# A selective scan on one core: delta transposed alone and multiplied with u by tokens; softplus in two ScalarE operations

## The chip, the cores and the metric

The kernel runs on one core of a Trainium2 chip. A core has five engines with an instruction stream each: TensorE (PE, matrix products and transposes into PSUM; its weight loads are shown as PEld), VectorE (DVE), ScalarE (ACT), GpSimd (POOL) and SyncE (SP), which here issues every DMA. Each engine works through its own stream in order; engines wait for each other through semaphores. The metric is the device time of one execution in microseconds (us), median over several runs. Everything is computed in 32-bit floats.

## The reference, cut to what matters

The input is a batch of eight images of 64 x 64 tokens with 192 channels. Two layers with residual follow each other. Layer 0 (a Mamba-2 block with convolutions and an MLP) is left alone by the change. Layer 1 is a selective scan in four directions:

```python
# layer 1; b images, L = 64*64 tokens, D_INNER = 384, D_STATE = 16, DT_RANK = 12, K = 4
xz = einsum('bhwc,dc->bhwd', group_norm(x), in_proj_w)
xc, z = split(xz, 2, axis=-1)
xc = silu(depthwise_conv3x3(xc) + conv_b)              # channels first
xs = stack([rows_first(xc), columns_first(xc)])        # two orders of the tokens
xs = concatenate([xs, flip(xs, axis=-1)])              # and both backwards: 4 directions
x_dbl = einsum('bkdl,kcd->bkcl', xs, x_proj_weight)    # 12 + 16 + 16 rows
dts, B, C = x_dbl[:, :, :12], x_dbl[:, :, 12:28], x_dbl[:, :, 28:]
delta = softplus(einsum('bkrl,kdr->bkdl', dts, dt_projs_weight) + dt_projs_bias)
A = -exp(A_logs)
def step(h, (d, b, c, u)):                             # token by token, u is xs
    h = exp(d[..., None] * A) * h + (d * u)[..., None] * b
    return h, sum_n(h * c)
y = sum over the directions, each turned back, of (scan(step) + xs * D)
out = x + (layer_norm(y) * silu(z)) @ out_proj_w.T
```

What the change touches is delta, the product d * u, and how the latter gets into the layout in which it is multiplied with B.

## The kernel before

Layer 0 runs over the eight images first and leaves its result in DRAM (`x1s`). Then layer 1 goes image by image. The 384 channels are three blocks of 128 (`DT`, index d), the 4096 tokens eight chunks of 512 (`NT`, index c or t).

For every image there is a **front**, a **scan** and a **finish**. The front of an image and the finish of the one before it are scheduled together by a small planner (`Flow`): each is a set of generators that yield steps with an engine, a weight in us and the instructions; the planner keeps a free time for each engine and emits the step that can start first. `take` and `give` are buffer slots, `wait` is an event, `fork` starts a further generator. The weights set only the order; on the chip the engines wait for data. The wait for "front" (line 1645) is where the prologue of the scan goes on when the whole front has been planned.

- Front (lines 1110 to 1235): load x1 (L1124), project to the inner channels (PE, L1139), copy into a padded image (ACT, L1169), convolve with nine taps on one ACT and eight DVE instructions of 128 x 4096 (L1190, L1200), silu in two halves (ACT, L1213), store by channels to DRAM as `xo[0]` (L1218), and turned to columns first (ACT copy L1227) as `xo[1]` (L1230). The weights scaled with the group norm of the image (`wxz`, L1100) lie in a pool that lives through the layer.
- Finish (lines 1237 to 1389): layer norm of `yacc` (PE means L1247, DVE L1255 and L1290, ACT L1265, L1283, L1284, L1297), the gate z (PE L1327, ACT L1345, DVE L1357), the output product (PE L1374), residual (DVE L1383) and store (L1386).

The scan of an image has 32 **steps** (4 directions k of 8 chunks; directions 2 and 3 backwards), and each step 24 **units**: eight pairs of states p times three channel blocks d. The main loop (`main`, line 1693) is written out by hand; in each engine the instructions stand in the order of the program. Unit u issues, in this order: `run(u)`, two DVE scans hs of 512 tokens (L1596) and on POOL the carry cy (L1608) and the product hc = hs * C (L1610); `decay(u + 2)`, two ACT exponentials ea (L1569); two or three `weigh`, ACT operations that multiply duT, delta * u with tokens on the partitions, with one column of B (pw, L1554); `supply(u + 1)`, eight PE transposes of pw into PSUM (g, L1580); `collect(u - 1)`, PE products that sum hc over the states (y, L1625); `add(u - 2)`, which adds y to `yacc` after the last pair (L1634, L1636). cb is C repeated over the partitions (DMA, L1542), dr is delta repeated (DMA, L1536).

While a step is scanned, the next one is prepared (`prepare`, line 1420): the table that it returns (line 1508) says in which of the 24 units each piece is issued. The pieces share a single PSUM bank, so each waits until the one before has been read. In unit 0 the chunk xc of `xo[k % 2]` is loaded (L1428); units 2 to 7 make dts, B and C (L1439 to L1462); then for each block d:

```python
step:    p_dt = wd^T x_dbl                        # PE, L1468
soft:    a = |p_dt|; a = exp(-a); a = ln(a + 1)   # ACT, L1475, L1476, L1477 (tile spa)
delta:   de = max(p_dt, 0) + a                    # DVE, L1482
times_u: du = de * xc                             # POOL, L1489
turn:    four transposes of du into PSUM (p_du)   # PE, L1495
keep_du: duT = p_du                               # DVE copy, L1502
```

For the first step of an image the same pieces run as generators of the planner (`prologue`, `prologue_of`, lines 1643 to 1691).

Of the kernel before, what the change touches and what calls it, by code (L numbers as in the profile page):

```python
# [8 lines left out]
F32 = mybir.dt.float32  # L9
AF = mybir.ActivationFunctionType  # L10
# [5 lines left out]
L = HI * WI  # L16
# [15 lines left out]
EXPLN = "natural_log_exp_and_others"  # L32

# [996 lines left out]
def layer1(tc, consts, x1s, mv1, out, w_in, w_x, w_dt, w_out):  # L1030
    nc = tc.nc
    ident, low, up, grp, eps, ones96, ones1, p96, p128 = consts
# [5 lines left out]
    with ExitStack() as ctx:  # L1038
# [48 lines left out]

        wxz = [wp.tile([CP, CT, DIN], F32, name=f"wi1{n}") for n in "xz"]

# [3 lines left out]
        def scaled(f, b, half):  # L1093

            for ct in range(CT):
                r = yield step(
                    "ACT",
                    0.6,
                    lambda: [
                        nc.scalar.activation(  # L1100
                            wxz[half][:, ct],
                            wi[:, ct, half * DIN : half * DIN + DIN],
                            AF.Copy,
                            scale=sc[:, b * CT + ct : b * CT + ct + 1],
                        )
                    ],
                )
            return r

        def front(f, cx, mq, b, xo):  # L1110

            fp = cx.enter_context(tc.tile_pool(name="fr1", bufs=1, reuse_waits="tile"))
            pads = [fp.tile([128, HI + 2, WI + 2], F32, name=f"pad{i}") for i in range(2)]
            for tag, n in (("xl", 3), ("fx", 2), ("pad", 2), ("xs", 2), ("xt", 1)):
                f.pool(tag, n)
            got = {}

            def load():
                for d in range(DT):
                    for t in range(NT):  # L1120
                        tk = slice(t * TT, t * TT + TT)
                        yield "take", "xl"
                        xl = got["xl", d, t] = fp.tile([CP, CT, TT], F32, name="xl1", bufs=3)
# [3 lines left out]
            def project():  # L1127
                yield from scaled(f, b, 0)
                for d in range(DT):
                    for t in range(NT):  # L1130
# [9 lines left out]
                                    ps, wxz[0][:, ct, d * 128 : d * 128 + 128], xl[:, ct], start=ct == 0, stop=ct == 1  # L1140
# [66 lines left out]
            def store():  # L1207
                for d in range(DT):
                    yield "wait", ("conv", d)
                    xs = got["xs", d]  # L1210
                    for h in range(2):
# [12 lines left out]
                        )  # L1224
                    yield "take", "xt"
                    xt = fp.tile([128, WI, HI], F32, name="xt1")
                    r = yield step("ACT", 7.2, lambda: [nc.scalar.copy(xt, xs.rearrange("p h w -> p w h"))])  # L1227
                    f.give("xs", r + 5)
# [4 lines left out]
                f.at["front"] = r  # L1233
# [3 lines left out]
        def finish(f, cx, mq, b):  # L1237

            fp = cx.enter_context(tc.tile_pool(name="fi1", bufs=1, side="right", reuse_waits="tile"))
            full = [128, DT, TT]  # L1240
            for tag, n in (("sq", 1), ("rs", 2), ("z", 2), ("xl2", 3)):
                f.pool(tag, n)
# [72 lines left out]
            def gate():  # L1315
                yield from scaled(f, b, 1)
                for t in range(NT):
                    yield "wait", ("xl2", t)
                    xl = got["xl2", t]
                    for d in range(DT):  # L1320
# [7 lines left out]
                                    ps, wxz[1][:, ct, d * 128 : d * 128 + 128], xl[:, ct], start=ct == 0, stop=ct == 1  # L1328
# [72 lines left out]
        def scan(xo):  # L1401
# [18 lines left out]
            def prepare(s, bank=lambda name: mp.tile([128, TT], F32, name=name, tag="mm")):  # L1420
# [5 lines left out]
                def load():  # L1426
                    st["xc"] = pools["pr1"].tile([128, DT, TT], F32, name="xc")
                    o(nc.sync.dma_start(out=st["xc"], in_=xo[k % 2][:, :, c * TT : c * TT + TT]))  # L1428
                    if first(s):
                        st["wd"] = pools["pr1"].tile([45, DIN], F32, name="wd")  # L1430
                        o(nc.sync.dma_start(out=st["wd"][32:45], in_=w_dt[k]))
                    else:
                        st["wd"] = state[s - 1]["wd"]
# [39 lines left out]
                def soft(d):  # L1473
                    st["sp", d] = a = pools["pr1"].tile([128, TT], F32, name="spa", tag="tmp")
                    o(nc.scalar.activation(a, st["p_dt", d], AF.Abs))  # L1475
                    o(nc.scalar.activation(a, a, AF.Exp, scale=-1.0))  # L1476
                    o(nc.scalar.activation(a, a, AF.Ln, bias=1.0))  # L1477

                def delta(d):
# [3 lines left out]
                            st["de", d], st["p_dt", d], 0.0, st["sp", d], ALU.max, ALU.add  # L1483
                        )
                    )

                def times_u(d):
                    st["du", d] = pools["pr1"].tile([128, TT], F32, name="du", tag="tmp")
                    o(nc.gpsimd.tensor_mul(st["du", d], st["de", d], st["xc"][:, d]))  # L1489

                def turn(d):
                    st["p_du", d] = pt = bank("p_du")
                    for j in range(NB1):
                        o(
                            nc.tensor.transpose(  # L1495
                                pt[:, j * 128 : j * 128 + 128], st["du", d][:, j * 128 : j * 128 + 128], ident
# [3 lines left out]
                def keep_du(d):  # L1500
                    o(
                        nc.vector.tensor_copy(  # L1502
                            st["duT"][:, :, d * 128 : d * 128 + 128],
                            st["p_du", d].rearrange("p (j t) -> p j t", j=NB1),
                        )
# [12 lines left out]
                    10: [(soft, 1), (times_u, 0)],  # L1518
                    11: [(delta, 1), (turn, 0), (repeat_delta, s, 0)],
                    12: [(keep_du, 0), (step, 2), (times_u, 1)],  # L1520
                    13: [(soft, 2)],
                    14: [(delta, 2), (turn, 1)],
                    15: [(keep_du, 1), (times_u, 2)],
# [148 lines left out]
            def prologue_of(f, d):  # L1672
# [5 lines left out]
                yield step("ACT", 1.9, lambda: ready["soft"](d), None, "explog")  # L1678
# [4 lines left out]
                yield "take", "tmp"  # L1683
                r = yield step("POOL", 1.3, lambda: ready["times_u"](d), r)
                yield "take", "mm"
                r = yield step("PE", 0.6, lambda: ready["turn"](d))
                f.give("tmp", r)
# [42 lines left out]
        for b in range(nb + 1):  # L1730
# [8 lines left out]
            if b < nb:  # L1739
                xo = [ddp.tile([128, DT, L], F32, name=f"xo{i}") for i in range(2)]  # L1740
                chains += front(f, fr_x, mq, b, xo)
# [16 lines left out]
def tile_kernel(ctx, tc, x, p96_in, p128_in, rows, w_in0, w_out0, w_fc1, w_fc2, w_in1, w_x, w_dt, w_out1, out):  # L1758
# [10 lines left out]
    for name in ("cw1", "cw2"):  # L1769
# [4 lines left out]
    low = cp.tile([128, 128], F32, name="low")  # L1774
    make_lower_triangular(nc, low, diag=False)
    up = cp.tile([128, 128], F32, name="up")
    nc.gpsimd.memset(up, 1.0)
    nc.gpsimd.affine_select(
        out=up, in_=up, compare_op=ALU.is_ge, fill=0.0, base=0, pattern=[[1, 128]], channel_multiplier=-1
    )  # L1780
# [5 lines left out]
    ones96 = cp.tile([CP, CP], F32, name="ones96")  # L1786
    nc.gpsimd.memset(ones96, 1.0 / C)
    ones1 = cp.tile([128, 128], F32, name="ones1")
# [3 lines left out]
    nb = x.shape[0]  # L1792
    mv1 = cp.tile([CP, nb, CT, 2], F32, name="mv1")
    x1s = [dp.tile([C, L], F32, name=f"x1_{b}") for b in range(nb)]
    layer0(tc, consts, x, x1s, mv1, w_in0, w_out0, w_fc1, w_fc2, rows)
    layer1(tc, consts, x1s, mv1, out, w_in1, w_x, w_dt, w_out1)
# [58 lines left out]
```

## Time and profile before

| | |
|---|---|
| runs | 24181.09, 24186.39, 24191.97 us; median 24186.39 |
| profiled execution | 24176.65 us, span 24174.9 us, mean granted PE clock 0.972 |
| busy share of the span | PE 87%, PEld 42%, DVE 88%, ACT 89%, POOL 70% |
| mean busy share of the 16 DMA engines | 23.4% |
| layer 0 | from the start to some 4861 us |
| scans of the first image | 5056 to 7220 us; the second 7456 to 9612 us |
| costliest groups (busy us, mean ns of one) | POOL hc L1610: 14577.7, 2373; DVE hs L1596: 13069.7, 1263; ACT pw L1554: 8875.8, 601; ACT ea L1569: 8123.2, 709; PE g L1580: 6793.2, 280; PE y L1625: 6658.3, 620 |
| loads and stores (KB each) | xc 768, xo<-xs 1024, xo<-xt 2048, cb 128, dr 128 |

How to read the lines that follow: a group is named by its line, engine, operation and `out<-in` (tiles without their numbers, partitions x elements), with the count after x; then come the busy time in us and the mean of one in ns, and the idle time of the engine just before these instructions with what ended it. A timeline has start and length in us. A window has, for each engine, busy us and the number of instructions in a stretch of the span. A wait has the waiting instruction, the one that released it, the total in us, how often, and the longest. Instructions of one engine overlap a little at their ends, so lengths add up to more than the time from one start to the next.

### The profile page before, as it was taken

The page shows a single profiled execution, that of the slowest core. Times are in us where ns is not written, and L with a number is a line of the kernel's source. Part 1 is how long each engine was busy: PE and PEld are TensorE (multiplying, and loading weights), DVE is VectorE, ACT ScalarE, POOL GpSimd, SP SyncE. Part 2 cuts the span into 40 slices and gives each one's busy share as a digit, 9 for nine tenths or more (in the row PEclk, how much of TensorE's full clock was granted, in tenths as well). Part 3 has the DMA queues.
Part 4 walks back from the last instruction along what each step waited for, and adds up shares of the span by engine and source line. Part 5 has one row for each costly group of instructions (what it writes and reads, how often), then busy time and mean ns, then how long its engine had stood idle before and what let it go on. Part 6 is the DMA issues. An engine that isn't in the chain of part 4 may idle for free.

```text
span 24174.9 us, 313055 instructions
## 1 busy us (share of the span) xinstructions
PE 20986.5 (87%) x100036; PEld 10182.8 (42%) x100036; DVE 21386.3 (88%) x22093; ACT 21415.5 (89%) x38076; POOL 16907.4 (70%) x13639
## 2 busy tenths in 40 slices
PE   7999999978888888888888888888888888888888
PEld 4444444434443444344434443444344434443444
DVE  7888888779998998899889988998899989998998
ACT  5666766679998999899989998999899989998998
POOL 1111111159986998699869986998699779977997
PEclk8999999989999999999999999999999999999999
DMA  2111111122222222222222222222222222222222
GB/s 49 44 44 44 49 44 42 36 86 67 68 66 87 68 67 68 89 66 66 69 87 68 68 68 86 67 68 70 84 68 67 76 78 67 68 75 82 67 67 58
DMA packets 1129702, 1608.05 MB, mean 67 GB/s; under 512 B 259360, under 2 KB 458432, under 8 KB 1118848
## 3 DMA queue, kind: packets, MB, share of 16 engines
q1 hardware_dynamic: 1128064, 1588.03, 23.4%
q8 instruction: 806, 13.21, 0.2%
q14 instruction: 832, 6.82, 0.1%
HBM read 1024.65 MB, written 160.17 MB: 49 GB/s over the span
## 4 chain that ended last, share of the span: by engine, by line
POOL 53%; PE 25%; issue 8%; DVE 6%; ACT 5%; DMA 2%; SPq 1%; POOLq 0%; DVEq 0%; ACTq 0%
POOL hc L1610 47%; POOL cy L1608 4%; PE y L1625 3%; PE p_f L953 3%; DVE xs L1200 3%; PE p_f L973 2%; PE p_x L445 2%; PE g L1580 2%; ACT pw L1554 2%; DMA xc<-xo 2%; PE p_o L870 1%; POOL du L1489 1%; ACT ea L1569 1%; PE p_y L787 1%; PE p_d L1439 1%
## 5 line engine op out<-in xcount | busy, mean ns | idle before, releaser
L1610 POOL TENSOR_TENSOR hc<-hs,cb 128x1024 f32<-128x1024 f32 x6144 | 14577.7, 2373 | 10.3 <-POOL cy L1608 6.7
L1596 DVE TENSOR_TENSOR_SCAN hs<-ea,cy,g 128x512 f32<-128x512 f32 x10752 | 13069.7, 1263 | 783.2 <-PE g L1580 468.3
L1554 ACT ACTIVATE pw<-duT,bt 128x384 f32<-128x384 f32 x16384 | 8875.8, 601 | 11.6 <-DVE duT L1502 11.6
L1625 PE MATMUL y<-hc,sel 128*64 128x512 f32 x24576 | 6658.3, 620 | 2229.1 <-POOL hc L1610 2221.3
L1569 ACT ACTIVATE ea<-dr,an 128x512 f32<-128x512 f32 x12288 | 8123.2, 709 | 159.9 <-DVE hs L1596 131.9
L1580 PEld LDWEIGHTS g<-ident,pw 128*128 128x128 f32 x49152 | 5309.6, 141 | 4320.1 <-issue 2676.5
L1580 PE MATMUL g<-ident,pw 128*128 128x128 f32 x49152 | 6793.2, 280 | 32.4 <-DVE hs L1596 12.9
L1625 PEld LDWEIGHTS y<-hc,sel 128*64 128x64 f32 x24576 | 1229.6, 135 | 3648.1 <-POOL hc L1610 3385.1
L1489 POOL TENSOR_TENSOR du<-de,xc 128x512 f32<-128x512 f32 x768 | 982.9, 1280 | 1632.9 <-DVE de L1482 1618.2
L1608 POOL COPY cy<-hs 128x2 f32<-128x2 f32 x6144 | 1161.7, 189 | 1324.4 <-DVE hs L1596 1211.9
L1596 DVE TENSOR_TENSOR_SCAN hs<-ea,g 128x512 f32<-128x512 f32 x1536 | 1777.0, 1204 | 178.7 <-PE g L1580 138.3
L362 POOL TENSOR_TENSOR s<-xs 96x512 f32<-96x512 f32 x64 | 121.0, 1891 | 2033.2 <-DVE xs L340 1522.3
L1200 DVE SCALAR_TENSOR_TENSOR xs<-pad,p,xs 128x4096 f32<-128x4096 f32 x192 | 860.8, 4484 | 37.6 <-ACT xs L1190 30.4
L1468 PE MATMUL p_dt<-xdbl,wd 13*128 13x512 f32 x1536 | 856.8, 639 | 41.7 <-DVE de L1482 39.7
L362 POOL TENSOR_TENSOR s<-sq 96x512 f32<-96x512 f32 x128 | 210.3, 1643 | 961.7 <-ACT sq L375 890.7
L1439 PE MATMUL p_d<-xc,wx 128*44 128x512 f32 x1536 | 792.2, 598 | 95.0 <-DMA xc<-xo 95.0
L340 DVE SCALAR_TENSOR_TENSOR x<-xx,p,x 96x512 f32<-96x512 f32 x1024 | 784.4, 814 | 19.4 <-ACT x L329 19.4
L953 PE MATMUL p_f<-h,wf 96*128 96x512 f32 x1536 | 764.1, 633 | 24.4 <-ACT zs L547 14.0
L340 DVE SCALAR_TENSOR_TENSOR xs<-xin,p,xs 96x512 f32<-96x512 f32 x1024 | 749.5, 768 | 4.6 <-ACT xs L329 4.6
L1482 DVE SCALAR_TENSOR_TENSOR de<-p_dt,spa 128x512 f32<-128x512 f32 x768 | 524.1, 682 | 254.0 <-ACT spa L1477 253.0
L973 PE MATMUL p_f<-m,wf 128*96 128x512 f32 x1536 | 693.3, 602 | 0.0
L1495 PEld LDWEIGHTS p_du<-ident,du 128*128 128x128 f32 x3072 | 323.1, 141 | 743.2 <-POOL du L1489 500.3
(201 smaller groups left out, 19729.0 us busy)
## 6 DMA issues: line engine op xcount, KB each, us to landing
cb<-cd SPq DMA_DIRECT2D x4096, 128.0 KB
dr<-de SPq DMA_DIRECT2D x3072, 128.0 KB
xc<-xo SPq DMA_DIRECT2D x256, 768.0 KB
e<-csd SPq DMA_DIRECT2D x256, 384.0 KB
xl<-x SPq DMA_DIRECT2D x256, 384.0 KB
xo<-xs SPq DMA_DIRECT2D x48, 1024.0 KB
xo<-xt SPq DMA_DIRECT2D x24, 2048.0 KB
xl<-in_x SPq DMA_DIRECT2D x64, 384.0 KB
```

The lines of the kernel that those rows point to most:

```text
L340: nc.vector.scalar_tensor_tensor(im(out[:, ct]), tap(ct, j), w[:, ct, j : j + 1], im(out[:, ct]), ALU.mult, ALU.add)
L953: nc.tensor.matmul(ps, wf1[:, ct, mt * 128 : mt * 128 + 128], h[:, ct], start=ct == 0, stop=ct == 1)
L973: nc.tensor.matmul(ps[:CP], wf2[:, kt, ct * CP : ct * CP + CP], m[:, kt], start=kt == 0, stop=kt == 5)
L1200: nc.vector.scalar_tensor_tensor(xs, tap(j), kw[:, d, j : j + 1], xs, ALU.mult, ALU.add)
L1489: o(nc.gpsimd.tensor_mul(st["du", d], st["de", d], st["xc"][:, d]))
L1554: nc.scalar.activation(st["pw", p, j][:, :, i], st["duT"][:, j].rearrange("p (g c) -> p g c", c=64), AF.Copy, scale=st["bt"][:, j, n : n + 1],
L1569: nc.scalar.activation(ea[:, f], state[s]["dr", d][:, f], AF.Exp, scale=an[:, k, p, at : at + 1])
L1580: nc.tensor.transpose(g[:, f, j * 128 : j * 128 + 128], state[s]["pw", p, j][:, 2 * d + f].rearrange("p a b -> p (a b)"), ident,)
L1596: nc.vector.tensor_tensor_scan(rev(h[:, f]), rev(ea[:, f]), rev(g[:, f]), 0.0 if first(s) else state[s - 1]["cy"][:, p, d, f : f + 1], ALU ...
L1608: o(nc.gpsimd.tensor_copy(st["cy"][:, p, d], h[:, :, last]))
L1610: o(nc.gpsimd.tensor_mul(hc, h, bc(st["cb", p], 1, [128, 2, TT])))
L1625: o(nc.tensor.matmul(y[half[f]], sel, hc[:, f], start=p == 0 and k > 0, stop=p == NP1 - 1))
```

## The change

For each image the front also writes u by tokens: after each silu half a generator `by_tokens` transposes it in groups of 512 tokens on PE, ACT copies each group out of PSUM, and SP stores it to a third DRAM tensor `xo[2]` of 4096 tokens x 384 channels. At each step `load` brings the chunk in as `ut`, tokens on the partitions, in the token order of the direction: one DMA in directions 0 and 2, two in directions 1 and 3, which go through the image by columns. `turn` transposes delta itself; `keep_du`, which was a copy out of PSUM, multiplies by `ut` on the way. `times_u` on POOL and its tile du are gone, and with them the entries of units 10, 12 and 15. softplus becomes Exp and Ln, ln(exp(v) + 1), on ACT; delta is max(min(that, 60), v).

Room in SBUF is made for it: the scaled weights go into pools of the front and of the finish, xl1 has two buffers in place of three, wd one in place of two, and the constants that only layer 0 uses are in a pool that is closed after layer 0.

```diff
 def layer1(tc, consts, x1s, mv1, out, w_in, w_x, w_dt, w_out):
...
-        wxz = [wp.tile([CP, CT, DIN], F32, name=f"wi1{n}") for n in "xz"]
...
         def front(f, cx, mq, b, xo):
...
+            wx_b = fp.tile([CP, CT, DIN], F32, name="wx1b")
...
-            for tag, n in (("xl", 3), ("fx", 2), ("pad", 2), ("xs", 2), ("xt", 1)):
+            for tag, n in (("xl", 2), ("fx", 2), ("pad", 2), ("xs", 2), ("xt", 1), ("xq", 2)):
...
-                        xl = got["xl", d, t] = fp.tile([CP, CT, TT], F32, name="xl1", bufs=3)
+                        xl = got["xl", d, t] = fp.tile([CP, CT, TT], F32, name="xl1", bufs=2)
...
+                        f.fork(by_tokens(d, h, xs, r))
                     yield "take", "xt"
                     xt = fp.tile([128, WI, HI], F32, name="xt1")
                     r = yield step("ACT", 7.2, lambda: [nc.scalar.copy(xt, xs.rearrange("p h w -> p w h"))])
-                    f.give("xs", r + 5)
+                    if last := f.part(("xs", d), 3, r + 5):
+                        f.give("xs", last)
...
-                f.at["front"] = r
+                if last := f.part("front", 2 * DT + 1, r):
+                    f.at["front"] = last
+
+            def by_tokens(d, h, xs, r):
+                xf = xs.rearrange("p h w -> p (h w)")
+                for g in range(h * NT // 2, h * NT // 2 + NT // 2):
+                    yield "take", "fx"
+                    ps = mq.tile([128, TT], F32, name="p_xq", tag="fx", bufs=2)
+                    r = yield step(
+                        "PE",
+                        0.6,
+                        lambda: [
+                            nc.tensor.transpose(
+                                ps[:, j * 128 : j * 128 + 128], xf[:, g * TT + j * 128 : g * TT + j * 128 + 128], ident
+                            )
+                            for j in range(NB1)
+                        ],
+                        max(r, f.now),
+                    )
+                    yield "take", "xq"
+                    xq = fp.tile([128, NB1, 128], F32, name="xq1", bufs=2)
+                    q = yield step("ACT", 0.6, lambda: [nc.scalar.copy(xq.rearrange("p j c -> p (j c)"), ps)], r)
+                    f.give("fx", q)
+                    dst = xo[2][g * TT : g * TT + TT, d * 128 : d * 128 + 128].rearrange("(j p) c -> p j c", p=128)
+                    q = yield step("SP", 0.1, lambda: [nc.sync.dma_start(out=dst, in_=xq)], q)
+                    f.give("xq", q + 2)
+                if last := f.part(("xs", d), 3, r):
+                    f.give("xs", last)
+                if last := f.part("front", 2 * DT + 1, q):
+                    f.at["front"] = last
...
                 def load():
                     st["xc"] = pools["pr1"].tile([128, DT, TT], F32, name="xc")
                     o(nc.sync.dma_start(out=st["xc"], in_=xo[k % 2][:, :, c * TT : c * TT + TT]))
+                    st["ut"] = pools["pr1"].tile([128, NB1, DIN], F32, name="ut", bufs=1)
+                    if k % 2 == 0:
+                        src = xo[2][c * TT : c * TT + TT].rearrange("(j p) m -> p j m", p=128)
+                        o(nc.sync.dma_start(out=st["ut"], in_=src))
+                    else:
+                        for i in range(2):
+                            src = xo[2].rearrange("(h w) m -> w h m", w=WI)[c * RT + i : c * RT + RT : 2]
+                            o(nc.sync.dma_start(out=st["ut"][i * 64 : i * 64 + 64], in_=src.rearrange("j h m -> h j m")))
...
                 def soft(d):
                     st["sp", d] = a = pools["pr1"].tile([128, TT], F32, name="spa", tag="tmp")
-                    o(nc.scalar.activation(a, st["p_dt", d], AF.Abs))
-                    o(nc.scalar.activation(a, a, AF.Exp, scale=-1.0))
+                    o(nc.scalar.activation(a, st["p_dt", d], AF.Exp))
                     o(nc.scalar.activation(a, a, AF.Ln, bias=1.0))
...
-                            st["de", d], st["p_dt", d], 0.0, st["sp", d], ALU.max, ALU.add
+                            st["de", d], st["sp", d], BIG, st["p_dt", d], ALU.min, ALU.max
...
-                def times_u(d):
-                    st["du", d] = pools["pr1"].tile([128, TT], F32, name="du", tag="tmp")
-                    o(nc.gpsimd.tensor_mul(st["du", d], st["de", d], st["xc"][:, d]))
...
-                                pt[:, j * 128 : j * 128 + 128], st["du", d][:, j * 128 : j * 128 + 128], ident
+                                pt[:, j * 128 : j * 128 + 128], st["de", d][:, j * 128 : j * 128 + 128], ident
...
-                        nc.vector.tensor_copy(
+                        nc.vector.tensor_mul(
                             st["duT"][:, :, d * 128 : d * 128 + 128],
                             st["p_du", d].rearrange("p (j t) -> p j t", j=NB1),
+                            st["ut"][:, :, d * 128 : d * 128 + 128],
...
-                    10: [(soft, 1), (times_u, 0)],
+                    10: [(soft, 1)],
                     11: [(delta, 1), (turn, 0), (repeat_delta, s, 0)],
-                    12: [(keep_du, 0), (step, 2), (times_u, 1)],
+                    12: [(keep_du, 0), (step, 2)],
                     13: [(soft, 2)],
                     14: [(delta, 2), (turn, 1)],
-                    15: [(keep_du, 1), (times_u, 2)],
+                    15: [(keep_du, 1)],
...
                 xo = [ddp.tile([128, DT, L], F32, name=f"xo{i}") for i in range(2)]
+                xo.append(ddp.tile([L, DIN], F32, name="xo2"))
```

## The prediction

> **What bounds the kernel now.** I read the busy shares of the page first: ACT 89%, DVE 88%, PE 87%. Averages so near each other name no limit, so I cut out a stretch of eighteen whole steps of the scan in one batch (directions 1 to 3) and asked the windows view for each engine's busy time in it.
>
> ```profile
> core 0: us, PE busy (x) PEld busy (x) DVE busy (x) ACT busy (x) POOL busy (x), PEclk, DMA share, GB/s
> 8344.90:9560.60 1215.70, 1042.80 (x5684) 512.62 (x5685) 1138.46 (x1062) 1208.94 (x2177) 1138.43 (x918) 1.00 0.24 67
> ```
>
> A step lasts 1215.70/18 = 67.54 us. Of it ACT works 67.16, DVE 63.25, POOL 63.25, PE 57.93. ACT has 0.38 us free in a step: it is the bound there. The chain of waits on the page puts 47% on the POOL product hc instead; POOL is idle 4.3 us in each step, so I believe the windows. The waits of the same stretch say how closely the others follow (releaser, us in total, times, longest):
>
> ```profile
> DVE hs L1596 <- PE g L1580: 40.2, 58, 1.5
> DVE de L1482 <- ACT spa L1477: 16.2, 34, 0.8
> DVE hs L1596 <- ACT pw L1554: 11.7, 17, 0.7
> DVE hs L1596 <- POOL cy L1608: 7.3, 17, 0.4
> ```
>
> DVE waits for ACT (16.2 + 11.7)/18 = 1.55 us in a step, and (40.2 + 7.3)/18 = 2.64 us for PE and POOL. The second sum doesn't go away with a faster ACT; it is the second floor: 63.25 + 2.64 = 65.89 us.
>
> Between two batches (some 235 us from the last scan to the next) ACT is not the bound:
>
> ```profile
> 7220.00:7300.00 80.00, 79.14 (x182) 34.23 (x182) 50.73 (x18) 44.87 (x49) 0.66 (x3) 0.98 0.42 114
> 7300.00:7387.00 87.00, 49.28 (x92) 18.10 (x92) 84.98 (x29) 45.92 (x34) 0.00 (x0) 0.82 0.35 131
> 7387.00:7456.00 69.00, 62.58 (x149) 24.26 (x150) 29.26 (x28) 50.08 (x63) 3.80 (x3) 0.93 0.46 143
> ```
>
> Columns as above. First PE (79 of 80), then the convolutions on DVE (85 of 87, PE free for 38 us), then PE again with 6 us free.
>
> **Part 1, softplus in two operations.** The timeline of ACT shows one softplus (start, duration):
>
> ```profile
> 8374.40 0.58 ACT L1475 ACTIVATE spa<-p_dt 128x512 f32<-128x512 f32 x1
> 8375.01 0.63 ACT L1476 ACTIVATE spa<-spa 128x512 f32<-128x512 f32 x1
> 8375.68 0.63 ACT L1477 ACTIVATE spa<-spa 128x512 f32<-128x512 f32 x1
> 8376.21 1.32 ACT L1569 ACTIVATE ea<-dr,an 128x512 f32<-128x512 f32 x2
> ```
>
> From its start to the next instruction's start it takes 8376.21 - 8374.40 = 1.81 us. Abs goes, and Exp reads PSUM in Abs's place. If Exp from PSUM lasts as Abs did, 0.61 us start to start are left before Ln: saved 0.66. If it keeps its own 0.63, saved 0.61. The group means below (575 against 630 ns) follow the place read, so I take 0.66: three a step, 1.98 us; the other end is 1.83. Over 256 steps that is 507 (468) us, if ACT stays the bound. The Trainium skill, page "ScalarE: Activation LUTs", section "What ACT_TABLE_LOAD costs", gives 186 ns + 0.833 ns an element and 93 ns of overlap with the next: an estimate of 0.52 us for the removed operation and 399 us in all; but the overlap it states is not there in these rows, where each operation needs the one before it, so the rows decide.
>
> ACT's floor becomes 67.16 - 1.98 + 0.38 = 65.56 us a step, DVE's is 65.89. The later one sets the step: 67.54 - 65.89 = **1.65 us saved**, not 1.98. Above it lies 1.98 (the 2.64 shrinks too, because POOL loses du, below). Below it I set 0.90 (16.2/18): the waits for spa go, those for pw only change their name to PE or POOL. The 32 steps of a batch include eight of the first direction, with two more PE products a unit; I give them the same. 256 x 1.65 = 422 us (230 to 507).
>
> **Part 2, the product with u moves from POOL to where delta leaves PSUM.** The rows of the groups view (busy, mean ns, idle before):
>
> ```profile
> L1489 POOL TENSOR_TENSOR du<-de,xc 128x512 f32<-128x512 f32 x768 | 982.9, 1280 | 1632.9 <-DVE de L1482 1618.2 <-PE p_du L1495 9.5 <-DMA dr<-de 5.2
> ...
> L1482 DVE SCALAR_TENSOR_TENSOR de<-p_dt,spa 128x512 f32<-128x512 f32 x768 | 524.1, 682 | 254.0 <-ACT spa L1477 253.0
> L1502 DVE COPY duT<-p_du 128x512 f32<-128x512 f32 x768 | 511.0, 666 | 8.1 <-PE p_du L1495 8.1
> ...
> L1475 ACT ACTIVATE spa<-p_dt 128x512 f32<-128x512 f32 x768 | 442.0, 575 | 69.8 <-PE p_dt L1468 69.6
> ...
> L1636 DVE TENSOR_TENSOR yacc<-yacc,y 128x512 f32<-128x512 f32 x576 | 382.0, 663 | 25.7 <-PE y L1625 25.7
> ```
>
> POOL loses 3 x 1.28 us a step. POOL is no bound, so directly nothing; but each du stands ahead of an hc, and PE's y waits for that hc. That is what can take the gain past 1.65, up to 1.98. DVE's copy (666 ns) becomes a product of a PSUM and an SBUF tensor; the addition into yacc has just these operands and this size and takes 663: price 0. The dearest row of a product of this size is du's own on POOL, 1280: that is the upper end, 3 x 0.61 = 1.84 us a step. I take 663, the same engine and operands. Max-add becoming min-max leaves delta at 682.
>
> The Trainium skill speaks against this edit: page "VectorE: DVE Perf Modes", section "Mode 2×_2P — use both read ports for one tensor", says that a copy can stream one tensor over both read ports and a two-tensor operation can't. By the headline alone a product would cost twice the copy, an estimate of 768 x 0.67 = 512 us on DVE, and the gain would be gone. The same section keeps the double rate to sources in SBUF; the copy here reads PSUM, and the trace has it at the addition's 666 against 663.
>
> delta is transposed directly, so PE's turn waits for DVE's de and no longer for POOL: same four transposes, earlier by 1.28. PE is in order, with y and g behind it, so this can only help. The new wait is keep_du's for ut; behind it on DVE stand the scans.
>
> **Part 3, ut from DRAM.** Each step loads 128 x 4 x 384 x 4 bytes = 768 KB more, as large as xc, with one SP issue (two in directions 1 and 3) of some 0.6 us. On the SP queue of the gap 2816 KB (xt, then xc) go from 7396.70, the issue of xt, to 7408.32, where the first piece of the chain below ends: 11.6 us, about 250 GB/s, so 3.2 us a step, 5% on a DMA share of 24%. It is issued in unit 0 of 24 and read in unit 12, 33 us later, and no cb load is due sooner than three units (8 us) after it: hidden, 0. Without that cover it would be 3.2 us a step.
>
> **Part 4, the front.** Each batch transposes xs for it: 24 groups of four PE transposes (0.65 us as p_du's), 24 ACT copies from PSUM (0.58), 24 stores of 256 KB. Two thirds belong to channel blocks 0 and 1 and fall under the next convolution, where PE has 38 us free and ACT 41: 0. The last eight groups come after the last silu, in the third window, where the chain reads:
>
> ```profile
> 7398.35 9.97 DMA xc<-xo
> ...
> 7408.46 1.91 PE p_d L1439 x2
> ...
> 7435.01 0.70 DVE duT L1502
> ...
> 7436.25 4.64 ACT pw L1554 x9
> ...
> 7443.89 10.55 PE p_o L1374 x24
> ```
>
> There they add 8 x 0.65 = 5.3 us of PE, 4.7 of ACT, and 2 MB (8.5 us at 250 GB/s) ahead of xc on the SP queue. Against that: xc has slack, since pw ends at 7440.9 and the first g waits for the p_o of the previous batch until 7454.4; PE is free 6 us; and the POOL stage of du leaves the chain (3 us, 7432 to 7435). Ends: 5.3 + 8.5 = +14 all exposed, -3 all covered. I take **+4**, near PE's share, since PE ends this window: 8 x 4 = 32 us. The first batch has no previous one to hide behind, and xl has two buffers in place of three: its eight projections go from some 1.9 us to (3.0 load + 1.9)/2 = 2.5 each, 5 more; with 1 for the later start of the weights 6 us, once. Constants moved to another pool issue nothing new: 0.
>
> **Sum.** The profiled execution took 24176.65 us (span 24174.9 and 1.75 around it): 24176.65 - 422 + 32 + 6 = 23793. It lay 9.7 under the median of the runs, so the forecast for the median is **23802 us**.
>
> **Rivals.**
> A: ACT keeps the bound and the front is covered: 24176.65 - 507 + 9.7 = 23679, with -3 us in each of eight batches 23655. For it: POOL's 3.8 us freed. Against: DVE's floor of 65.89.
> B: DVE, PE and POOL close the gap: 0.90 a step (230) and +14 a batch (118): 24176.65 - 230 + 118 + 9.7 = 24074. For it: DVE's waits for g, 2.2 us a step, are the largest already. Against: the spa and pw waits name ACT.
> C, slower: the product at L1502 costs more on DVE than the addition shows. DVE's floor rises by three times the excess; the gain of 1.65 less the front's 38/256 = 0.15 is used up at 0.50 us each, that is from 1.17 us for one product. At du's 1280 ns: 1.84 - 1.65 + 0.15 = +0.34 a step, 87 us: 24273. For it: no product of these operands exists yet. Against: L1636.
> D: the change doesn't do what it says: Exp from PSUM lasts as long as Abs and Exp did together. Then only the front's 38 us are left: 24224. Against: ACT reads p_dt from PSUM in 575 ns now, and Exp from SBUF takes 630.
>
> **Chances.** Forecast 0.58 (its own range 23690 to 23920), A 0.12, B 0.17, C 0.10, D and what lies between B and no change 0.03. Range 23650 to 24060: A's best to near B's end. A measurement of this kernel tells about 0.2% (48 us) from no change: faster 0.84 (forecast, A and most of B), same 0.06, slower 0.10.
>
> **What would show it.** In the same stretch: a step of 65.9, ACT at 65.2 or nearly full, the spa and pw waits under half, L1502 near 665, no ut among the releasers of DVE; after the last silu eight transposed groups and the first scan some 4 us later than now. A step above 67, a product over 1.2 us, or a DMA wait at keep_du would make it wrong.

## The result and the profile after

| | median of the runs, us | lowest to highest | ratio to the kernel before, 95% interval |
|---|---|---|---|
| before | 24187.47 (4 runs) | 24181.09 to 24191.97 | |
| after | 23754.53 (4 runs) | 23741.9 to 23765.26 | 0.9821 (0.9809 to 0.9833) |

The change saves 433 us, 1.8%. The forecast was 23802, 47 us above. The profiled execution of after took 23759.13 us, its span 23757.4 against 24174.9: 417.6 us less. The instruction records give these parts of the difference:

| part of the span | before | after | difference | forecast |
|---|---|---|---|---|
| eight scans, first to last scan instruction of an image | 8 x 2164.7 | 8 x 2101.1 | -509 | -422 |
| seven gaps between two scans | 7 x 238.7 | 7 x 249.0 | +72 | +28 |
| start of the first scan | 5049.5 | 5067.5 | +18 | +10 |
| after the last scan | 137.0 | 138.3 | +1 | 0 |

By these records the first image's scan before runs from 5049.5 to 7217.1 us and the second's from 7456.5 to 9620.4. Of the 18 us, 6.6 already lie ahead of layer 1, which starts at 4861.5 us before and at 4868.1 in after; in a second run of after it starts at 4847.0, so this lies within the spread of layer 0 between runs and is none of the change's. Both large terms were missed, in opposite directions.

The windows view of after, for eighteen whole steps of directions 1 to 3 in one batch (columns: us, then busy time and instructions of PE, PEld, DVE, ACT and POOL, the PE clock, the DMA share, GB/s):

```profile
8286.40:9466.70 1180.30, 1039.59 (x5690) 512.54 (x5690) 1131.87 (x1063) 1175.85 (x2126) 1080.42 (x864) 1.00 0.31 81
```

A step is 1180.30/18 = 65.57 us, 1.97 less than the 67.54 of the same view before. ACT works 65.32 of it, DVE 62.88, POOL 60.02. By this line alone ACT, 99.6% full, is still the bound; the run without Ln below shows that a second limit lies just beside it. The waits view of the same stretch (us in total, times, longest):

```profile
PE y L1663 <- POOL hc L1648: 134.0, 252, 1.1
POOL cy L1646 <- DVE hs L1634: 90.2, 210, 1.0
...
DVE hs L1634 <- PE g L1618: 35.2, 52, 1.3
...
DVE hs L1634 <- POOL cy L1646: 6.8, 16, 0.4
...
DVE hs L1634 <- ACT pw L1592: 2.7, 5, 0.8
DVE hs L1634 <- ACT ea L1607: 1.5, 3, 0.5
```

PE's y waits 134.0 us for hc, against 163.3 before. The waits of DVE for spa are gone and those for pw fell from 11.7 to 2.7. What is left of DVE's waits is 46.2/18 = 2.57 us a step; with its 62.88 busy that is 65.45, a hair under the step. No ut stands among the releasers. The groups of the changed operations, in the groups view of the whole span (busy us, mean ns of one, idle before):

```profile
L1539 DVE TENSOR_TENSOR duT<-p_du,ut 128x512 f32<-128x512 f32 x768 | 510.1, 666 | 1.2 <-PE p_du L1532 1.2
...
L1258 ACT COPY xq<-p_xq 128x512 f32<-128x512 f32 x192 | 110.5, 584 | 168.6 <-DMA xo<-xq 167.7 <-PE p_xq L1249 0.2
```

The product costs DVE what the copy cost, 666 ns. The new copies of the front, however, wait 167.7 us for their stores, over the eight images. The gap between the first two images, in the windows view with the cuts about where one image's PE stage ends and the convolutions end:

```profile
7174.00:7252.00 78.00, 78.00 (x179) 33.88 (x176) 48.13 (x18) 43.57 (x52) 0.49 (x3) 0.97 0.40 106
7252.00:7342.00 90.00, 64.86 (x166) 28.59 (x165) 87.73 (x29) 57.16 (x50) 0.00 (x0) 0.81 0.53 182
7342.00:7422.00 80.00, 69.94 (x177) 29.25 (x177) 28.05 (x28) 53.13 (x69) 0.00 (x0) 0.87 0.52 159
```

The first two windows are about as long as before (80 and 87); the third, after the last convolution, was 69 us and is 80. The instruction records say the same without hand-made cuts, as means of the seven gaps: from the last scan instruction to the end of the convolutions 165.5 us against 167.1 before, and from there to the next scan 83.5 against 71.6. So the whole lengthening lies behind the last convolution. No engine is full in the third window. Its chain of waits shows who sets it:

```profile
7344.44 6.67 DMA xo<-xq
...
7352.53 8.74 DMA xo<-xq
...
7369.81 6.13 DMA xc<-xo
```

Two stores of transposed groups, 15 us together, now stand in the chain ahead of the load of xc.

### The profile page after: what moved, and what is told of

Same layout as the page of the kernel before. It is cut to its first block, busy times and chain, and to the rows that moved or that the text cites. A ratio compares the mean times of both kernels' runs of the same rounds, so it can differ in the third digit from the quotient of the medians.

```text
span 23757.4 us, 313126 instructions
## 1 busy us (share of the span) xinstructions
PE 21089.6 (89%) x100804; PEld 10279.5 (43%) x100804; DVE 21274.2 (90%) x22093; ACT 21040.0 (89%) x37507; POOL 16067.4 (68%) x12871
## 4 chain that ended last, share of the span: by engine, by line
POOL 43%; PE 24%; ACT 15%; DVE 7%; issue 6%; DMA 4%; SPq 1%; POOLq 0%; ACTq 0%; DVEq 0%
POOL hc L1648 40%; ACT pw L1592 6%; ACT ea L1607 6%; POOL cy L1646 3%; PE p_f L956 3%; DMA xc<-xo 2%; DVE xs L1202 2%; PE p_f L976 2%; PE p_x L448 2%; PE y L1663 2%; PE p_o L873 2%; PE p_y L790 1%; PE g L1618 1%; PE p_d L1481 1%; PE p_z L531 1%
## 5 line engine op out<-in xcount | busy, mean ns | idle before, releaser
L1532 PEld LDWEIGHTS p_du<-ident,de 128*128 128x128 f32 x3072 | 323.5, 141 | 610.2 <-DVE de L1523 405.8
L448 PE MATMUL p_x<-h,wi 96*128 96x512 f32 x1024 | 544.5, 664 | 12.3 <-ACT h L405 11.1
L365 POOL TENSOR_TENSOR s<-x 96x512 f32<-96x512 f32 x64 | 96.2, 1502 | 626.3 <-DVE x L343 477.2
```

## Experiments

Each kernel ran beside the kernel before on the same chip; ratios are to that. "Step" is the median in directions 1 to 3, "scan" the mean of the eight images' scans, "gap" the mean of the seven gaps.

| run | median us | ratio, 95% interval | step | scan | gap |
|---|---|---|---|---|---|
| before | 24162 to 24191 in four sets of runs | 1 | 67.64 | 2164.7 | 238.7 |
| after | 23754.53 | 0.9821 (0.9809 to 0.9833) | 65.57 | 2101.1 | 249.0 |
| softplus alone (e1) | 24080.99 | 0.9963 (0.9948 to 0.9978) | 67.16 | 2149.2 | 243.3 |
| move alone (e2) | 24201.65 | 1.0013 (1.0003 to 1.0022) | 67.34 | 2157.6 | 248.9 |
| after, again | 23747.24 | 0.9824 (0.9807 to 0.984) | 65.56 | 2101.3 | 250.0 |
| softplus alone, du not awaited (e8) | 24093.41 | 0.9969 (0.9958 to 0.9981) | 67.16 | 2152.2 | 242.9 |
| the same, half of du (e15) | 23821.18 | 0.9845 (0.9828 to 0.9861) | 66.24 | 2117.3 | 242.9 |
| after without Ln (e6) | 23699.04 | 0.9805 (0.9791 to 0.982) | 65.55 | 2095.9 | 249.3 |
| after, ut loaded once (e9) | 23759.48 | 0.9818 (0.9803 to 0.9833) | 65.57 | 2100.4 | 250.3 |
| after, four xq buffers (e3) | 23703.71 | 0.9807 (0.9792 to 0.9821) | 65.57 | 2100.6 | 245.2 |
| the same again (e3b) | 23710.31 | 0.9801 (0.9786 to 0.9815) | 65.57 | 2100.9 | 245.0 |
| after, xt on POOL's queue (e5) | 23743.79 | 0.9826 (0.9811 to 0.9841) | 65.56 | 2100.2 | 249.2 |
| after, u by tokens of one image (e4) | 23694.68 | 0.9802 (0.9787 to 0.9816) | 65.57 | 2100.4 | 241.1 |

### The two halves of the change, each alone

The first takes the kernel before and changes nothing but the softplus and the weight of its step in the planner (e1). The second is the changed kernel with the softplus of three operations put back (e2).

```diff
 # e1, on the kernel before
-                    o(nc.scalar.activation(a, st["p_dt", d], AF.Abs))
-                    o(nc.scalar.activation(a, a, AF.Exp, scale=-1.0))
+                    o(nc.scalar.activation(a, st["p_dt", d], AF.Exp))
...
-                            st["de", d], st["p_dt", d], 0.0, st["sp", d], ALU.max, ALU.add
+                            st["de", d], st["sp", d], 60.0, st["p_dt", d], ALU.min, ALU.max
...
-                yield step("ACT", 1.9, lambda: ready["soft"](d), None, "explog")
+                yield step("ACT", 1.3, lambda: ready["soft"](d), None, "explog")
```

> The kernel before with softplus in two ScalarE operations alone; the product with u stays on POOL and there is no ut. Theory 1, ScalarE alone: a step follows ScalarE's work, wherever the product stands, so a step falls from 67.5 to about 65.6 us and the gap between two images stays at some 238 us: 24187 - 256 x 2.0 = about 23675, some 80 us faster than the changed kernel. Theory 2, the move frees the step: with du on POOL, VectorE's floor of 65.89 us holds, so a step takes 65.9 to 66.0: 24187 - 256 x 1.6 = about 23775, no better than the changed kernel.

> The changed kernel with the three ScalarE operations of softplus and the max-add put back: the move of the product alone. Theory 1: a step stays at ScalarE's 67.5 us and only the longer gaps are left, 7 x 10 + 11 us more than before: about 24270. Theory 2: POOL's 3.8 us a step relieve VectorE and PE, a step falls by 0.3 to 0.5 us: 24187 - 256 x 0.4 + 82 = about 24165, no slower than before.

Neither theory of e1 was right: at 67.16 us a step it is slower than both. e2 came out between its two theories, 31 us slower than the kernel before on its chip (24170.65), with a step of 67.34. Softplus alone gives 15.5 us a scan, 0.48 a step. The move alone gives 7.1 us a scan, and its dearer gaps eat that. Both together give 63.6 us a scan; 41 of them, 328 us over eight images, appear only when both are there. The windows view of e1, then of e2, eighteen steps each:

```profile
8252.10:9461.20 1209.10, 1039.91 (x5690) 515.53 (x5690) 1135.61 (x1063) 1185.92 (x2125) 1139.69 (x918) 1.00 0.24 68
```

```profile
8284.40:9497.00 1212.60, 1053.48 (x5690) 511.63 (x5692) 1133.77 (x1063) 1208.61 (x2180) 1079.07 (x864) 1.00 0.30 79
```

In e2 ACT works 1208.61 of 1212.60 us: it is the bound, as it was before. In e1 no engine is full. ACT has 23.2 us free in eighteen steps (1209.10 - 1185.92), its busy time fell by 1.28 us a step, and the step by 0.48. (The operations are those of after: the groups' busy times add up to 1262.3 us here and to 1261.0 in the stretch of after. Where ACT waits they overlap less, so its busy time is longer, 65.88 against 65.32 a step.) DVE works 63.09 us a step and POOL 63.32, as before the change. The waits of e1 tell where the step goes:

```profile
DVE hs L1595 <- PE g L1579: 49.4, 52, 2.0
...
ACT ea L1568 <- DVE hs L1595: 16.4, 37, 0.6
...
DVE hs L1595 <- ACT pw L1553: 13.0, 21, 1.6
```

DVE waits for g more than before (49.4 against 40.2 us, single waits up to 2.0 against 1.5), and ACT, which waited 0.9 us for DVE in the stretch before, now waits 16.4. One such wait, in the timeline of e1 (start, length, engine, line; the idle time before it in brackets):

```profile
8283.13 1.28 POOL L1488 TENSOR_TENSOR du<-de,xc 128x512 f32<-128x512 f32 x1
...
8284.49 2.37 POOL L1609 TENSOR_TENSOR hc<-hs,cb 128x1024 f32<-128x1024 f32 x1
...
8286.92 1.08 PE L1624 MATMUL y<-hc,sel 128*64 128x512 f32 x4 [0.92 <-POOL hc L1609]
...
8287.93 1.12 PE L1468 MATMUL p_dt<-xdbl,wd 13*128 13x512 f32 x2
...
8288.98 1.09 PE L1579 MATMUL g<-ident,pw 128*128 128x128 f32 x8
...
8290.21 1.28 DVE L1595 TENSOR_TENSOR_SCAN hs<-ea,cy,g 128x512 f32<-128x512 f32 x1 [1.29 <-PE g L1579]
```

Read it downward. du pushes hc back by 1.28 us; y, the next work on PE, waits 0.92 for that hc; p_dt and then g stand behind y; the scan waits 1.29 for g. After the du at 8283.13 POOL runs without an idle moment until 8295.47. Two explanations remain, and both fit this picture: POOL's time ahead of hc, or the wait of the turn, and so of duT, for du itself.

### GpSimd's time, or the wait for du

e8 is e1 with delta transposed in place of du: GpSimd still computes du at the same place, but nothing reads it. The scan's input is then without u. e15 does the same with a du of half the columns.

```diff
 # e8, on e1
-                                pt[:, j * 128 : j * 128 + 128], st["du", d][:, j * 128 : j * 128 + 128], ident
+                                pt[:, j * 128 : j * 128 + 128], st["de", d][:, j * 128 : j * 128 + 128], ident
 # e15, on e8
-                    o(nc.gpsimd.tensor_mul(st["du", d], st["de", d], st["xc"][:, d]))
+                    o(nc.gpsimd.tensor_mul(st["du", d][:, :256], st["de", d][:, :256], st["xc"][:, d, :256]))
```

> The softplus alone (as in the run e1_soft_only: 67.16 us a step, 24081 in all), with GpSimd's product delta*u still computed at the same place and for the same time, but PE transposing delta itself, so that nothing waits for the product; the scan input is left without u. Theory 1: it is GpSimd's 3 x 1.1 us of time ahead of the x10 products that hold the softplus alone at 67.16: step stays at 67.0 to 67.2, total 24060 to 24090. Theory 2: it is the turn's wait for the product (latency on the way to VectorE's copy of duT): step falls to about 65.6, total about 23680.

> As e8_du_unread, but GpSimd multiplies only the first 256 of 512 columns, so that it loses about half of 3.3 us a step ahead of the x10 products. The whole product costs 1.6 us a step (67.16 against 65.57). Theory 1: GpSimd has slack for the first 1.6 us and each further one is paid in full: step 65.5 to 65.8, total about 23690. Theory 2: every microsecond of it costs about half a one: step 66.3 to 66.5, total about 23890.

In e1 the turn (p_du) waits 37.5 us for du in the eighteen steps. In e8 the waits view has no such wait, and DVE waits for g as long as in e1:

```profile
DVE hs L1595 <- PE g L1579: 51.1, 52, 2.3
...
PEld p_du L1494 <- DVE de L1481: 28.4, 35, 0.8
```

With the turn free of du, the step is 67.16, that of e1 (the scans are 3.0 us longer, 2152.2 against 2149.2). So it is GpSimd's time, and theory 2 of e8 falls. A third possibility, that DVE's own operations run slower while GpSimd works, is small: DVE works 63.09 us a step in e8 and 62.88 in after. The windows view of e8, then of e15:

```profile
8257.00:9468.50 1211.50, 1042.16 (x5690) 517.93 (x5690) 1135.57 (x1063) 1186.85 (x2125) 1139.64 (x918) 0.99 0.24 68
```

```profile
8210.80:9401.10 1190.30, 1034.94 (x5690) 513.64 (x5692) 1132.98 (x1063) 1177.82 (x2125) 1113.67 (x918) 1.00 0.24 69
```

POOL works 63.31 us a step in e8, 61.87 in e15 and 60.02 in after. Here after stands for no du at all; it is another kernel, but its product on DVE takes as long as the copy did, and the load of ut costs the step nothing (e9, below). From after to e15 POOL's work grows by 1.85 us and the step, by the scans' means, by (2117.3 - 2101.1)/32 = 0.51. From e15 to e8 it grows by 1.44 and the step by (2152.2 - 2117.3)/32 = 1.09. Neither theory of e15 was right, 66.24 being nearest to the second: by these three points each further microsecond costs more than the one before. The first part is taken mostly out of POOL's idle time, which falls from 5.55 us a step in after (1180.30 - 1080.42, over 18) to 4.26 in e15; from there to e8 it falls only to 3.99, and three quarters of the added work lengthen the step.

### What stands next under ScalarE

```diff
 # e6, on the changed kernel: delta is left without the logarithm
-                    o(nc.scalar.activation(a, a, AF.Ln, bias=1.0))
```

> The changed kernel without the logarithm (L1518, three times 631 ns a step): delta is left without it. Shows what stands next under ScalarE. Theory 1: ScalarE, full to 65.3 of 65.57 us, is the only bound, and the step falls with it by 1.9 us to about 63.8, the total by about 460 us to 23290. Theory 2: VectorE with its waits for PE and GpSimd (62.9 busy and 2.3 waiting) stands right under it: step 65.2, total about 23660. Values in between say how far the waits shrink.

Three operations of 631 ns less on ACT, and a scan falls by 5 us, 0.16 a step, not by 1.9. Theory 2 holds, with a floor of 1178.30/18 = 65.46 us in the stretch below rather than 65.2. The windows and the waits of e6:

```profile
8162.30:9340.60 1178.30, 1032.91 (x5690) 513.30 (x5690) 1132.01 (x1063) 1155.82 (x2072) 1079.56 (x864) 1.00 0.31 81
```

```profile
DVE hs L1633 <- PE g L1617: 25.2, 35, 1.3
...
ACT ea L1606 <- DVE hs L1633: 15.3, 36, 0.7
...
DVE hs L1633 <- ACT pw L1591: 11.1, 21, 0.8
```

ACT has 22.5 us free in this stretch and waits for DVE. DVE's waits are again about 2.5 us a step, as in after. So in after two limits stand together: ACT's work at 65.32, and DVE's work with its waits, which comes to 65.46 even with less work on ACT.

### The load of ut

```diff
 # e9, on the changed kernel: one chunk of u serves all steps of an image, so 31 of 32 multiply by the wrong tokens
-                    st["ut"] = pools["pr1"].tile([128, NB1, DIN], F32, name="ut", bufs=1)
-                    if k % 2 == 0:
+                    if s == 0:
+                        st["ut"] = pools["pr1"].tile([128, NB1, DIN], F32, name="ut", bufs=1)
...
-                        for i in range(2):
-                            src = xo[2].rearrange("(h w) m -> w h m", w=WI)[c * RT + i : c * RT + RT : 2]
-                            o(nc.sync.dma_start(out=st["ut"][i * 64 : i * 64 + 64], in_=src.rearrange("j h m -> h j m")))
+                        st["ut"] = state[s - 1]["ut"]
```

> The changed kernel with the 768 KB of u by tokens loaded in the first step of an image alone and read again in the other 31; delta is then multiplied with the wrong tokens of u. Theory 1: the load is hidden at all times: step 65.5 to 65.6 as before, total within 20 us of the changed kernel (23750 beside a kernel before of 24175). Theory 2: it crowds the load of xc, which stands in the chain of waits with 4.4 to 5.5 us a step: step 65.4 or less, total 40 to 100 us lower.

The step stays at 65.57 and the total within its own spread, while the DMA share of the stretch falls from 0.31 to 0.25. Theory 1: the load is hidden.

### The gap

```diff
 # e3, on the changed kernel
-            for tag, n in (("xl", 2), ("fx", 2), ("pad", 2), ("xs", 2), ("xt", 1), ("xq", 2)):
+            for tag, n in (("xl", 2), ("fx", 2), ("pad", 2), ("xs", 2), ("xt", 1), ("xq", 4)):
...
-                    xq = fp.tile([128, NB1, 128], F32, name="xq1", bufs=2)
+                    xq = fp.tile([128, NB1, 128], F32, name="xq1", bufs=4)
 # e4, on the changed kernel: u by tokens is written for the first image and used for all eight
...
-                        f.fork(by_tokens(d, h, xs, r))
+                        if b == 0:
+                            f.fork(by_tokens(d, h, xs, r))
...
 # e5, on the changed kernel
-                        "SP", 0.1, lambda: [nc.sync.dma_start(out=xo[1][:, d], in_=xt.rearrange("p w h -> p (w h)"))], r
+                        "POOL", 0.1, lambda: [nc.gpsimd.dma_start(out=xo[1][:, d], in_=xt.rearrange("p w h -> p (w h)"))], r
```

> The changed kernel with four buffers for xq in place of two. Theory: the gap grew because ScalarE waits for the store of xq to leave one of two buffers, 6 us of it behind the 2 MB store of xt in the last channel block; with four the gap falls by about 5 us for each image: 23754 - 8 x 5 = about 23715. Rival: what counts is the added work of PE and ScalarE and the bytes ahead of xc on the SP queue; then nothing changes, 23750.

> The changed kernel, but u by tokens is written for the first image alone and its tensor is read by all the others: seven times the transposes, copies and stores of the front are left out. Theory: the longer gaps are these; they fall from 249 us to 238 or a little less (the POOL stage of du has left the prologue): 23754 - 7 x 11 = about 23675, and the first image is as before. Rival: the gaps grew through the smaller edits, two buffers for xl1 and the weights scaled in the pools of the front and the finish; then they stay above 245 us and the time at 23740 or more.

> The changed kernel itself, once more, as the yardstick for the runs beside it on this chip: 23754 us expected (its earlier runs spread from 23742 to 23765), 65.57 us a step, 249 us between two scans.

> The changed kernel, with the 2 MB store of the turned image (xt) issued on POOL's DMA queue, so that the small stores of u by tokens no longer stand behind it on SP's. Theory 1: the copies into xq (L1258) wait because their stores are queued behind xt on SP; then their idle time (168 us in all) falls to under 60, a gap falls from 249 to about 244 us, and the total by about 35 us, as four buffers for xq did. Theory 2: the 16 DMA engines are shared, so the small stores wait behind xt's packets whichever queue issues them: idle time and total within 10 us of the changed kernel. Theory 3: an issue on POOL costs POOL time ahead of the products that PE waits for, and the scan next to it gets slower: step above 65.7.

> The changed kernel with four buffers for xq instead of two, once more, on another chip than the first time: ratio 0.981 again (0.9807 the first time, against 0.9821 to 0.9824 of the changed kernel), gaps of 245 us.

Without the tokens the gap is 241.1 us: they cost 249.0 - 241.1 = 7.9 of the 10.3 us, so the theory of e4 holds for most of it. Four buffers take back 4 of these, as the theory of e3 said. The instruction records show the place: the first product of the next scan's preparation (p_d, which needs xc) starts 37.1 us after the last convolution, in the mean of the gaps, against 24.0 before and 32.1 with four buffers. The copies' row in the groups view of e3, then of e5:

```profile
L1258 ACT COPY xq<-p_xq 128x512 f32<-128x512 f32 x192 | 107.3, 586 | 83.9 <-DMA xo<-xq 63.0 <-PE p_xq L1249 18.1 <-ACT xq L1258 2.1
```

```profile
L1258 ACT COPY xq<-p_xq 128x512 f32<-128x512 f32 x192 | 110.3, 583 | 174.6 <-DMA xo<-xq 171.0 <-PE p_xq L1249 2.9
```

With four buffers the copies wait 63.0 us for stores in place of 167.7. With xt's 2 MB store on another queue they wait 171.0, no less: the queue is not what the small stores stand behind, and theory 1 of e5 falls; theory 3 falls with the step of 65.56. The Trainium skill, "DMA: Bandwidth & Descriptors", section "Issuing engines are not separate DMA queues", says that whichever engine starts them, DMAs run on the same 16 DMA engines and interleave. The row of e5 agrees with it. Whether xt's bytes delay the small stores at all is not shown: no run leaves xt out.

Some 2 us of the gap are not the tokens' (241.1 against 238.7), and e1, e8 and e15, whose fronts are untouched, have 243.3, 242.9 and 242.9. In e1 the longer part lies behind the first p_d: from there to the first scan it takes 52.0 us against 47.6 before. Whether the shorter softplus does this or the order that the planner makes of its new weight wasn't tried and stays open.

The four buffers make the fastest of these kernels that leaves nothing out: 0.9807 and 0.9801 on two chips. Their intervals overlap that of after; for the difference speak the gaps, and on the second chip the runs (23704.25 to 23727.93), which lay below those of e9 (23740.59 to 23763.74), a kernel that times like the changed one.

## Why the prediction was right, and where it was not

**Softplus, size of the operation: right.** ACT's work fell from 67.16 to 65.32 us a step, 1.84, at the low end of the 1.83 to 1.98 worked out from the rows. Exp from PSUM took 576 ns, as Abs had, so the reason for taking 1.98 held and the size was 0.14 too large. (By the rows one softplus keeps 0.61 of 1.28 us, which saves 0.67, not 0.66.)

**The step of 65.9 and its cause: the time nearly right, the reason wrong.** The prediction took DVE's work and its waits for PE and POOL, 2.64 us, as a fixed second floor of 65.89 and gave the whole 1.65 us to the softplus. e1 shows the floor that was really there: 67.16. With ACT out of the way DVE's waits for PE and POOL grew from 2.64 to (49.4 + 9.5)/18 = 3.27 us, 9.5 being its waits for cy, and those for pw did not go away. A sum of waits seen while another engine is the bound is not the floor behind it.

**The failed step: "POOL loses 3 x 1.28 us a step. POOL is no bound, so directly nothing".** Taking du from POOL was worth (2152.2 - 2101.1)/32 = 1.60 us a step, once the softplus was shorter. Idle time of 4.3 us a step was the argument, as a mean over the step. By the instruction records, 1.8 us of DVE's waits in a step of e1 end between 17 and 35 us after the step's bt copy, and 0.1 in after. 1.4 of them end at 18 to 20 us, as the wait in the timeline above does, which follows the first du by way of hc and y. (The three du start 11.6, 17.7 and some 26.6 us after that copy.) Between 12 and 36 us POOL is idle 0.28 us of its 3.86 a step in e1: it was a bound there and idle elsewhere. The prediction saw the path (du ahead of hc, y behind hc) and used it only as the upper end of the gain. The two errors, a floor too low for the softplus and a price of nothing for the move, cancelled because both edits came together; that is luck, not foresight.

**Between 1.65 and 1.98.** Measured 1.99 a step over all scans (63.6/32): rival A's step, for A's stated reason, POOL's time set free. A's other half, a front that costs nothing, did not come, and neither did B's 0.90 a step.

**The product on DVE: right.** 666 ns against 663 forecast; rival C is out. Rival D is out by ACT's 1.84 us.

**The load of ut: right.** e9 prices it at nothing in the step.

**The front: mis-sized.** Forecast +4 us a gap, measured +10.3. Its step "two thirds ... fall under the next convolution ...: 0" held: the part up to the last convolution is 1.6 us shorter than before (165.5 against 167.1). What was mis-sized are the last eight groups, put near PE's share of 5.3: the part behind the last convolution is 11.9 us longer. The prediction counted PE's and ACT's time and the stores' bytes, 8.5 us for all eight, about 1 us each, but not the return of the two xq buffers: a copy waits until an earlier store of 256 KB has landed, and the two stores in the chain above take 6.67 and 8.74 us. e3 puts half of the tokens' cost there; the rest of it was not split further. The dear end, 14, named the stores; the value taken lay near the middle between it and -3. (The 250 GB/s left out a load of 384 KB that stands between xt and xc on the queue, so it was too low.)

The first image came out near: counted from the start of layer 1, its first scan came 11.4 us later, against 10. But the reason is only in part the one given, the loads and weights: with four xq buffers 4.9 of these us are gone.

**The sum.** The scans gave 87 us more than forecast (509 against 422), the rest took 53 more (72 + 18 + 1 = 91 against 38, layer 0's 6.6 among them): 34 us of the span. The other 14 or so of the 47 by which the forecast was too high come from the runs profiled: that of before lay 9.7 under the median taken, that of after 4.6 above its own. So the total is near because of two cancellations: scans against gaps, and within the scans the softplus against the move.

The Trainium skill, "Perfetto Trace Analysis", section "Identifying the Most-Contended Engine", finds the bottleneck by occupancy and says to improve that engine first. This case agrees only half. ACT at 99.4% of a step was the bound before, but taking 1.28 us a step of busy time off it gave only 0.48 (e1); in after it is at 99.6%, and three Ln of 0.63 us less gave 0.16 (e6).

## What to carry to other kernels

An engine with a few us free in a step can still be the bound of a stretch of that step: look at where its idle time lies, and at what stands ahead of the operation that others wait for, before pricing work on it at nothing. When two resources lie within a per cent of each other, try removing work from both in one change: each edit alone can look almost worthless, as here (0.48 and 0.22 us a step, against 1.99 for both). For copies that leave through DMA, count the time until a buffer comes back as well as the engines' work.

## What the runs showed of the hardware

GpSimd's product took 736 ns for 128 x 256 elements (e15) and 1282 for 128 x 512 (e1). If the time grows evenly with the columns, an estimate from these two sizes, 2 x 736 - 1282 = 190 ns do not depend on the size. VectorE's product of a PSUM and an SBUF tensor took 666 ns at 128 x 512, as its copy out of PSUM did (666). Moving the issue of a 2 MB store from SP to POOL changed neither the wait of the stores beside it (171.0 against 167.7 us) nor the step.
